# The last 255 attention logits moved to the border of two PSUM banks, and the padded column set by GpSimd, in a planned two-layer graph kernel

## The chip, the cores and the metric

The kernel runs on one core of one Trainium2 chip. The metric is the device time of one execution in microseconds, as the median of three runs. All arithmetic that this document speaks of is in fp32.

## The reference

The input is a matrix `x` of 3327 nodes by 256 features and a weighted adjacency matrix `adj` of 3327 by 3327. Two layers follow one another, each with a layer norm and a ReLU in front and a residual addition behind. The first one is what the change touches:

```python
def _top_p_attention(X, W1, W2, W3):
    q = X @ W1.T @ W2.T                    # 3327 x 64
    k = X @ W3.T                           # 3327 x 64
    logits = q @ k.T / TAU
    probs = jax.nn.softmax(logits, axis=-1)
    idx = jnp.argsort(-probs, axis=-1)
    sp = jnp.take_along_axis(probs, idx, axis=-1)
    cs = jnp.cumsum(sp, axis=-1)
    keep_sorted = cs - sp < TOP_P          # 0.9
    ...
    A = probs * mask
    return A / jnp.maximum(A.sum(-1, keepdims=True), 1e-12)
...
for n in range(STEPS):                     # 2
    A = _top_p_attention(Xa, W1, W2, W3)
    Xf = R @ Xf                            # R: row-normalised adj + I
    Xa = A @ Xa
    Z = Z + Xf @ U1[n].T + Xa @ U2[n].T
```

So for every node there are 3327 logits against all nodes; their exponentials are thinned to the largest that hold 0.9 of the sum, and what is left weighs the rows of `Xa`. The second layer is a graph attention with four heads over the neighbours that `adj` names.

## The kernel before, in words

The 3327 nodes are padded to 3328 (`NP`), which is 26 row tiles (`NT`) of 128. Thus exactly one node, the last of the last tile, is padding, and in every row of logits there is exactly one padded column, number 3327 (`N`).

**One row tile of attention** is an object of class `Row` (from L854). Its pieces run on all engines. `logits` (L873) makes the 128 x 3327 logits on TensorE in four portions of up to 1024 columns. Only 64 features are contracted, so the keys `kt` lie in two halves of the partitions: portion k holds 512 keys in partitions 0 to 63 and another 512 in partitions 64 to 127, and two matmuls (r = 0 and r = 1, L882) of 64 rows each fill the two banks of a PSUM tile `pl` of two banks. The last portion, k = 3, has only 255 columns: 128 for r = 0 at the start of the first bank, and 127 for r = 1 at the start of the second. For the padded 128th column of the second bank there is one more matmul, L890, of one column: its operands come from a constant tile `none` and make a logit of -32,000, whose exponential is zero. `exps` (L893) then takes one activation per portion on ScalarE, from PSUM to the SBUF tile `e` of 3328 columns, with the sum beside it; for k = 3 it reads 2 x 128 columns.

After that come the sum (`row_sum`), a guess of the threshold (`root` on GpSimd, `guess` and `density` on ScalarE), two or three counts over the 3327 columns on ScalarE (`count`, L933) with small steps on GpSimd or VectorE between them (`step`), a windowed search for the largest values on VectorE (`window`, L981; `sort`; `choose`, L1013), two small GpSimd operations between them (`free`, L995, lines L997 and L998), and four passes over `e` on VectorE that zero what falls below the threshold (`drop`, L1040). All of these read or write columns below 3327 only. Then TensorE transposes `e` in seven groups (`turn`, L1051; transposes at L1056), six of four and the last of two 128 x 128 blocks: the last transposed block, columns 3200 to 3327, holds the padded column. ScalarE copies each group out of PSUM (`turned`, L1061), and TensorE multiplies the blocks with the features (`attend`, L1068). Both steps have 26 such row tiles, 52 in all.

**Beside the attention** each step has 26 products with rows of the adjacency matrix (class `Full`: `some`, L1100, 26 matmuls of 128 x 128 by 256 or 257, fed by loads on SP's queue; `copy`, L1107, takes the result out of PSUM on ScalarE), and projections at the start (`project_u`, L1218) and after each row tile (`finish1`, `finish2`). The second layer's main loops are L1644 (VectorE), L1632 and L1633 (ScalarE), L1660 and L1674 (TensorE).

**The order of all this** is not written out by hand. Class `Plan` (L470) holds pieces, each with an engine, a length in microseconds that the author put in, a rank, the pieces it needs, and the buffers it takes and gives back. `order` (L497) simulates the five engines with these lengths: whenever an engine is free, it takes the piece of lowest rank among those whose needs and buffers are there. `issue` then emits the instructions in that order, and on the chip each engine works through its own queue in it. A length is thus no time on the chip, but it decides which piece comes before which, on all engines. The two logits pieces of a row (portions 0 and 1, then 2 and 3) are put at L1429 to L1431 with lengths 2.1 and 1.4, `free` at L1459 with length 0.8 (on GpSimd). Some pieces do nothing and only pass a buffer on; the one at L1223, put once for each of 26 tiles in `project_u`, has length 0.0 and lag 0.0 on SP.

In `order`, what a piece releases goes into a heap of events with a time (`finish`, L502). The loop handles all events up to the current time, lets each engine take a piece, and then moves the clock to the earliest later time at which an engine with waiting pieces is free, or at which the first event of the heap is due:

```python
times = [t for e, t in now.items() if t > clock and ready[e]] + ([events[0][0]] if events else [])
later = [t for t in times if t > clock]
```

Of the kernel before, what the change touches and what calls it, by code (L numbers as in the profile page):

```python
# [10 lines left out]
F32 = mybir.dt.float32  # L11
# [8 lines left out]
P = 128  # L20
N = 3327
# [3 lines left out]
DA = 64  # L25
# [444 lines left out]
class Plan:  # L470
# [26 lines left out]
    def order(self):  # L497
        free, events = dict(self.free), []
        now = dict.fromkeys(self.LAG, 0.0)
        ready = {e: [] for e in self.LAG}  # L500

        def finish(p, end):  # L502

            heapq.heappush(events, (end, p["k"], p, "own"))
            heapq.heappush(events, (end + p["lag"], p["k"], p, ""))
            for b in p["give"]:
                heapq.heappush(events, (end + p["lag"], p["k"], p, b))

        for k, p in enumerate(self.pieces):
            p["k"], p["left"], p["from"] = k, len(p["needs"]), 0.0  # L510
            if not p["left"]:
                ready[p["engine"]].append(p)
        out, clock, holds = [], 0.0, []
        while len(out) < len(self.pieces):
            while events and events[0][0] <= clock:
                _, _, p, what = heapq.heappop(events)
                if what == "end":

                    held = sum(max(0.0, min(z, clock) - max(a, p["at"])) for a, z in holds[-12:])
                    end = p["at"] + p["length"] + held  # L520
                    if end > clock + 1e-6:
                        now[p["engine"]] = end
                        heapq.heappush(events, (end, p["k"], p, "end"))
                    else:
                        finish(p, clock)
                    continue
                if what not in ("", "own"):
                    free[what] += 1
                    continue
                for q in p["then"]:  # L530
                    if (q["engine"] == p["engine"]) == (what == "own"):
                        q["left"] -= 1
                        if not q["left"]:
                            ready[q["engine"]].append(q)
            for e, queue in ready.items():
                if now[e] > clock or not queue:
                    continue
                can = [p for p in queue if all(free[b] >= p["take"].count(b) for b in p["take"])]
                if not can:
                    continue  # L540
                p = min(can, key=lambda q: q["rank"])
                queue.remove(p)
                for b in p["take"]:
                    free[b] -= 1
                p["at"] = clock
                now[e] = clock + p["length"]
                if p["hold"]:
                    holds.append((clock, clock + p["hold"]))
                if e == "POOL":
                    heapq.heappush(events, (now[e], p["k"], p, "end"))  # L550
                else:
                    finish(p, now[e])
                out.append(p)
            times = [t for e, t in now.items() if t > clock and ready[e]] + ([events[0][0]] if events else [])
            later = [t for t in times if t > clock]
            if not later:
                if len(out) < len(self.pieces):
                    raise RuntimeError("the plan stands still")
                break
            clock = min(later)  # L560
        self.end = max(now.values())
        return out
# [8 lines left out]
def fast(  # L571
# [59 lines left out]
    with ExitStack() as l0:  # L631
# [16 lines left out]
        kt = wpool.tile([P, 3 * 512 + P], F32, name="kt")  # L648
        qq = wpool.tile([P, NT, P], F32, name="qq")


        none = wpool.tile([P, P + 2], F32, name="none")
        GP.memset(none, 0.0)
        GP.memset(none[DA : DA + 32, :P], 1.0)
        GP.memset(none[DA : DA + 32, P:], -1.0e3)
        kks = [wpool.tile([P, P + 2], F32, name=f"kk{k}") for k in range(2)]
        for kk in kks:
            GP.memset(kk[:, :: P + 1], 1.0)
# [195 lines left out]
        class Row:  # L854
# [18 lines left out]
            def logits(self, k):  # L873

                if k == 0:
                    self.open()
                pl = ps_l.tile([P, 2, 512], F32, name="pl")
                w = 512 if k < 3 else P
                for r in range(2):
                    m = min(w, N - 1024 * k - w * r)  # L880
                    half = slice(r * DA, r * DA + DA)
                    T.matmul(  # L882
                        pl[:, r, :m],
                        qq[half, self.i, :],
                        kt[half, 512 * k : 512 * k + m],
                        start=True,
                        stop=True,
                    )
                    if m < w:
                        T.matmul(pl[:, r, m:w], none[half, :P], none[half, P : P + w - m], start=True, stop=True)  # L890
                self.pl[k] = pl[:, :, :w]

            def exps(self, k):  # L893
                pl = self.pl.pop(k)
                w = pl.shape[2]
                S.activation(  # L896
                    self.e[:, 1024 * k : 1024 * k + 2 * w].rearrange("p (r w) -> p r w", r=2),
                    pl,
                    AF.Exp,
                    accum_out=(self.p0, self.p1, self.p2, self.p3)[k],  # L900
                )
# [93 lines left out]
            def free(self):  # L995

                GP.tensor_scalar(self.room, self.h0, self.h1, self.b, ALU.add, ALU.subtract)  # L997
                GP.tensor_scalar(self.rec, self.s, self.h0, self.h1, ALU.subtract, ALU.subtract)  # L998

            def sort(self):  # L1000

# [417 lines left out]
        def search(row, rank, keys, stats_of, fresh):  # L1419


            n, i = row.n, row.i
            got, a = [], None
            for g in range(2):

                def logits(g=g):
                    row.logits(2 * g)
                    row.logits(2 * g + 1)

                a = plan.put(  # L1430
                    "PE", 2.1 - 0.7 * g, rank - 2.5, logits, needs=[keys, fresh, a], take=["pl", "pl"] + ["e", "sc"] * (1 - g)  # L1431
                )
                for k in (2 * g, 2 * g + 1):
                    got.append(
                        plan.put("ACT", 1.15 if k < 3 else 0.5, rank - 2.5, row.exps, k, needs=[a], give=["pl"])
                    )
            row.pieces = dict(logits=a)
            a = plan.put("ACT", 0.35, rank - 2.4, row.row_sum, needs=[got])
            a = plan.put("POOL", 1.3, rank - 2.4, row.root, needs=[a, stats_of])
            a = row.pieces["guess"] = plan.put("ACT", 1.0, rank - 2.4, row.guess, needs=[a])  # L1440
            more = plan.put("ACT", 0.85, rank - 2.2, row.density, needs=[a])
            for j in range(2):
                got = [
                    plan.put("ACT", 3.05, rank - (2.1, 1.7)[j], row.count, j, fn, needs=[a])
                    for fn in (AF.Relu, AF.Sign)[j:]
                ]
                a = plan.put("POOL", (3.8, 4.7)[j], rank - (2.0, 1.6)[j], row.step, j, GP, needs=[got, more])
            if EVALS[n] == 3:
                a = row.pieces["counted"] = plan.put("ACT", 3.05, rank - 1.4, row.count, 2, AF.Sign, needs=[a])
                a = plan.put("DVE", 2.7, rank - 1.3, row.step, 2, V, needs=[a])  # L1450
            halves = []
            for h in range(2):
                for part in range(2):
                    a = plan.put(
                        "DVE", 3.2 - 2.0 * part, rank - 1.0, row.window, h, part, needs=[a], take=["y"] * (1 - part),
                        give=["y"] * part, lag=0.02, hold=1.95 * (1 - part),
                    )
                    halves.append(a)
            may = plan.put("POOL", 0.8, rank - 1.5, row.free, needs=[halves[2]])  # L1459
            a = plan.put("DVE", (1.8, 2.5)[n], rank - 1.0, row.sort, needs=[a])  # L1460
            a = plan.put("DVE", 3.1, rank - 1.0, row.choose, needs=[a, may], take=["cum"])
            total = plan.put("POOL", 1.2, rank - 1.0, row.total, needs=[a], give=["cum"])
            drops = []
            for o in range(4):
                a = plan.put("DVE", 1.03, rank - 1.0, row.drop, o, needs=[a], hold=1.0)
                drops.append(a)
            return total, drops
# [504 lines left out]
```

## Time and profile before

| what | value |
|---|---|
| median of 3 runs | 2207.8 us (2207.56 to 2210.33) |
| the profiled execution: its own time | 2208.77 us |
| the profiled execution: its span in the trace | 2207.0 us |
| instructions in the trace | 35945 |
| VectorE busy | 1614.3 us (73%) |
| ScalarE busy | 1443.2 us (65%) |
| GpSimd busy | 932.8 us (42%) |

The span is from the first to the last instruction of the program in the trace; 1.77 us of the execution's own time lie around it. A group line of the profile names the source line, the engine, the operation, the written and read tiles, the shape and the count, then the summed busy time, the mean duration of one in ns, and the idle time before them with what ended it. PE is TensorE's matmuls, PEld its weight loads, DVE VectorE, ACT ScalarE, POOL GpSimd, SP the engine that issues DMAs. An fp32 matmul of the program shows up as two matmul instructions, called passes below, so that 52 matmuls of the source are 104 in the trace; the transposes at L1056 show up once.

By place, the attention steps with their adjacency products fill the trace up to about 1720 us, the second layer the rest: the first second-layer matmul at L1660 starts at 1722.25 us.

### The profile page before, as it was taken

What the parts mean: (1) busy time and instruction counts of PE and PEld (TensorE: products, weight loads), DVE (VectorE), ACT (ScalarE), POOL (GpSimd) and SP (SyncE); (2) the same over time, 40 slices, a digit from 0 to 9 for tenths busy, and PEclk for the clock granted to TensorE, in tenths of its full rate; (3) what the DMA queues carried; (4) which work ended last, traced back from release to release, by engine and by line L of the source; (5) the groups of instructions that cost most, each with busy time, mean ns of one, the idle gap of its engine ahead of it and who ended that gap; (6) DMA issues with size and microseconds to landing.
All of it is one profiled execution on the core that took longest, in us unless ns stands there. A gap on an engine that the chain in (4) does not pass through costs nothing. (4 is left out here: it accounts for less than half of the span.)

```text
span 2207.0 us, 35945 instructions
## 1 busy us (share of the span) xinstructions
PE 2169.5 (98%) x11978; PEld 1530.4 (69%) x11978; DVE 1614.3 (73%) x4229; ACT 1443.2 (65%) x2726; POOL 932.8 (42%) x2210
## 2 busy tenths in 40 slices
PE   8999999999999999999999999999999999999997
PEld 6488778778877788878777888878888433333332
DVE  5566757546665573177979798787778997989896
ACT  5776776566666751478787878778764555455553
POOL 5554465435454550255665656666663100000001
PEclk9999999999999999999999999999999999999999
DMA  4012121212212232532212222222224444444341
GB/s 120 1 45 85 49 70 50 75 52 61 73 49 76 65 92 80 185 84 63 67 55 62 60 72 71 77 63 63 71 77 143 137 126 138 116 141 124 110 128 52
DMA packets 192323, 183.75 MB, mean 83 GB/s; under 512 B 15386, under 2 KB 146176, under 8 KB 192128
## 3 DMA queue, kind: packets, MB, share of 16 engines
q1 hardware_dynamic: 191232, 181.15, 28.3%
q8 instruction: 96, 1.57, 0.3%
q14 instruction: 99, 0.81, 0.1%
q10 hardware_dynamic: 896, 0.21, 0.0%
HBM read 164.41 MB, written 15.94 MB: 82 GB/s over the span
## 5 line engine op out<-in xcount | busy, mean ns | idle before, releaser
L1068 PE MATMUL acca<-rhs,et 128*128 128x256 f32 x2704 | 616.8, 379 | 0.0
L933 ACT ACTIVATE junk<-e,sc 128x3327 fp8e5<-128x3327 f32 x182 | 559.0, 3071 | 68.3 <-POOL sc L978 67.6
L1068 PEld LDWEIGHTS acca<-rhs,et 128*128 128x128 f32 x2704 | 499.3, 190 | 62.5 <-issue 1.5
L1100 PE MATMUL accf<-c,at 128*128 128x256 f32 x1352 | 316.8, 383 | 4.7 <-ACT f L1107 4.5
L1100 PE MATMUL accf<-main,at 128*128 128x257 f32 x1352 | 310.9, 381 | 1.0 <-ACT f L1107 0.5
L988 DVE SCALAR_TENSOR_TENSOR y<-e,sc 128x1664 f32<-128x1664 f32 x104 | 208.9, 2009 | 131.6 <-POOL sc L975 129.6
L1100 PEld LDWEIGHTS accf<-c,at 128*128 128x128 f32 x1352 | 248.7, 190 | 51.0 <-issue 10.6
L1100 PEld LDWEIGHTS accf<-main,at 128*128 128x128 f32 x1352 | 250.8, 190 | 46.1 <-issue 9.4
L1061 ACT COPY et<-px 128x512 f32<-128x512 f32 (+1 forms) x364 | 192.3, 553 | 125.0 <-PE px L1056 69.8
L993 DVE MAX8 cands<-y 128x8 f32<-128x208 f32 x832 | 242.2, 361 | 3.6
L1043 DVE SCALAR_TENSOR_TENSOR e<-e,thr 128x832 f32<-128x832 f32 x208 | 213.0, 1079 | 1.8
L896 ACT ACTIVATE e<-pl 128x1024 f32<-128x1024 f32 x208 | 179.8, 868 | 42.0 <-PE pl L882 41.7
L1633 ACT ACTIVATE et<-at 128x448 bf16<-128x448 f32 (+1 forms) x204 | 112.3, 550 | 129.1 <-DVE e L1644 75.8
L1056 PE MATMUL px<-ident,e 128*128 128x128 f32 x1352 | 190.8, 274 | 5.4 <-ACT et L1061 2.5
L1796 POOL TENSOR_TENSOR qq<-qq 128x256 f32<-128x256 f32 x4 | 3.0, 754 | 452.3 <-ACT qq L1792 452.2
L1660 PE MATMUL pl<-e,main 128*64 128x416 f32 x1024 | 191.3, 517 | 0.2
L1056 PEld LDWEIGHTS px<-ident,e 128*128 128x128 f32 x1352 | 159.4, 141 | 45.4 <-issue 13.5
L882 PE MATMUL pl<-kt,qq 64*128 64x512 f32 (+1 forms) x832 | 173.5, 535 | 0.0
L1660 PEld LDWEIGHTS pl<-e,main 128*64 128x64 f32 x1024 | 70.8, 137 | 112.2 <-issue 87.1
L1644 DVE SCALAR_TENSOR_TENSOR e<-c,low,et 128x832 f32<-128x832 f32 x128 | 128.5, 1072 | 8.6 <-PE accf L1674 7.0
L882 PEld LDWEIGHTS pl<-kt,qq 64*128 64x128 f32 x832 | 71.6, 186 | 83.6 <-issue 80.3
L1644 DVE SCALAR_TENSOR_TENSOR e<-qq,low,et 128x832 f32<-128x832 f32 x120 | 120.5, 1075 | 6.0 <-PE accf L1674 4.4
(528 smaller groups left out, 3080.0 us busy)
## 6 DMA issues: line engine op xcount, KB each, us to landing
at<-in_adjt_dram SPq DMA_DIRECT2D x414, 256.0 KB
at<-in_adjt_dram SPq DMA_DIRECT2D x102, 192.0 KB
at<-in_adjt_dram SPq DMA_DIRECT2D x52, 128.0 KB
ys<-ystage SPq DMA_DIRECT2D x26, 256.0 KB
rhs<-in_x_dram SPq DMA_DIRECT2D x26, 128.0 KB
ystage<-in_x_dram SPq DMA_DIRECT2D x26, 128.0 KB
base<-ys SPq DMA_DIRECT2D x26, 128.0 KB
x1s<-ystage SPq DMA_DIRECT2D x26, 128.0 KB
```

Source lines behind the costliest of these rows:

```text
L882: T.matmul(pl[:, r, :m], qq[half, self.i, :], kt[half, 512 * k : 512 * k + m], start=True, stop=True,)
L896: S.activation(self.e[:, 1024 * k : 1024 * k + 2 * w].rearrange("p (r w) -> p r w", r=2), pl, AF.Exp, accum_out=(self.p0, self.p1, self.p2 ...
L933: S.activation(junk[:, :N], self.e[:, :N], fn, bias=t, scale=-1.0, accum_out=dst, saturate=False)
L988: V.scalar_tensor_tensor(self.y[:, : hi - lo], self.e[:, lo:hi], self.up, self.e[:, lo:hi], ALU.is_lt, ALU.mult, accum_out=(self.h0, self. ...
L993: V.max(self.cands[:, o // PIECE, :], self.y[:, o - lo : min(o + PIECE, hi) - lo])
L1043: V.scalar_tensor_tensor(piece, piece, self.thr[:, o : o + 1], piece, ALU.is_gt, ALU.mult)
L1056: T.transpose(pt[:, k, :], self.e[:, j * P : (j + 1) * P], ident)
L1061: S.copy(self.et[g][:, :m, :], self.pt.pop(g)[:, :m, :])
L1068: T.matmul(self.acc, et[:, j - 4 * g, :], rhs[self.n][:, j, :], start=(j == 0), stop=(j == NT - 1))
L1100: T.matmul(self.acc[:, : self.w], self.at[j // JC][:, j % JC, :], self.src[:, j, : self.w], start=(j == 0), stop=(j == NT - 1),)
L1644: V.scalar_tensor_tensor(held["e"][:, k, :], extra["both"][b % 2][:, k, :], low[:, j, k : k + 1], held["mask"], ALU.max, ALU.mult,)
L1660: T.matmul(q["acc"][a][k * FH : (k + 1) * FH, c, :C], main[:, j, h * FH : (h + 1) * FH], held["e"][:, h, c * C : (c + 1) * C], start=(j == 0),
```

## The change

The change has four parts. The one-column matmul at L890 and the constant tile `none` with its three memsets go. The last portion of logits lies differently in its PSUM tile: the 128 columns of r = 0 are the last 128 of the first bank, and the 127 of r = 1 the first 127 of the second, so that the 255 columns lie one behind the other across the border of the banks, and the activation reads 255 columns as one stretch (the other portions lie as before). Since nothing writes column 3327 of `e` any more, GpSimd sets it to zero at the end of `free`. In the plan, the lengths of the two logits pieces become 2.0 and 1.2, and `order` handles events that fall due at the current time before it moves the clock.

```diff
--- before.py
+++ after.py
@@ -551,6 +551,8 @@
                 else:
                     finish(p, now[e])
                 out.append(p)
+            if events and events[0][0] <= clock:
+                continue
             times = [t for e, t in now.items() if t > clock and ready[e]] + ([events[0][0]] if events else [])
             later = [t for t in times if t > clock]
             if not later:
@@ -648,11 +650,6 @@
         kt = wpool.tile([P, 3 * 512 + P], F32, name="kt")
         qq = wpool.tile([P, NT, P], F32, name="qq")
 
-
-        none = wpool.tile([P, P + 2], F32, name="none")
-        GP.memset(none, 0.0)
-        GP.memset(none[DA : DA + 32, :P], 1.0)
-        GP.memset(none[DA : DA + 32, P:], -1.0e3)
         kks = [wpool.tile([P, P + 2], F32, name=f"kk{k}") for k in range(2)]
         for kk in kks:
             GP.memset(kk[:, :: P + 1], 1.0)
@@ -876,25 +873,25 @@
                     self.open()
                 pl = ps_l.tile([P, 2, 512], F32, name="pl")
                 w = 512 if k < 3 else P
+
+                pl = pl.rearrange("p r w -> p (r w)")
                 for r in range(2):
                     m = min(w, N - 1024 * k - w * r)
                     half = slice(r * DA, r * DA + DA)
+                    lo = 512 - w + w * r
                     T.matmul(
-                        pl[:, r, :m],
+                        pl[:, lo : lo + m],
                         qq[half, self.i, :],
                         kt[half, 512 * k : 512 * k + m],
                         start=True,
                         stop=True,
                     )
-                    if m < w:
-                        T.matmul(pl[:, r, m:w], none[half, :P], none[half, P : P + w - m], start=True, stop=True)
-                self.pl[k] = pl[:, :, :w]
+                self.pl[k] = pl[:, 512 - w : lo + m]
 
             def exps(self, k):
                 pl = self.pl.pop(k)
-                w = pl.shape[2]
                 S.activation(
-                    self.e[:, 1024 * k : 1024 * k + 2 * w].rearrange("p (r w) -> p r w", r=2),
+                    self.e[:, 1024 * k : 1024 * k + pl.shape[1]],
                     pl,
                     AF.Exp,
                     accum_out=(self.p0, self.p1, self.p2, self.p3)[k],
@@ -996,6 +993,8 @@
 
                 GP.tensor_scalar(self.room, self.h0, self.h1, self.b, ALU.add, ALU.subtract)
                 GP.tensor_scalar(self.rec, self.s, self.h0, self.h1, ALU.subtract, ALU.subtract)
+
+                GP.memset(self.e[:, N:], 0.0)
 
             def sort(self):
 
@@ -1428,7 +1427,7 @@
                     row.logits(2 * g + 1)
 
                 a = plan.put(
-                    "PE", 2.1 - 0.7 * g, rank - 2.5, logits, needs=[keys, fresh, a], take=["pl", "pl"] + ["e", "sc"] * (1 - g)
+                    "PE", 2.0 - 0.8 * g, rank - 2.5, logits, needs=[keys, fresh, a], take=["pl", "pl"] + ["e", "sc"] * (1 - g)
                 )
                 for k in (2 * g, 2 * g + 1):
                     got.append(
```

## The prediction, made before the changed kernel was run

> **What bounds the kernel now.** I read the first part of the page, then busy time by stage, then TensorE's waits, and then single instructions.
>
> ```profile
> PE 2169.5 (98%) x11978; PEld 1530.4 (69%) x11978; DVE 1614.3 (73%) x4229; ACT 1443.2 (65%) x2726; POOL 932.8 (42%) x2210
> ```
>
> Busy time by stage (columns: stretch, its length, then PE, PEld, DVE, ACT and POOL busy, clock, DMA share, GB/s):
>
> ```profile
> 60.00:120.00 60.00, 55.74 (x192) 29.41 (x193) 38.78 (x117) 45.78 (x86) 29.83 (x73) 1.00 0.00 1
> 120.00:1720.00 1600.00, 1588.89 (x8074) 1289.82 (x8073) 1101.97 (x3445) 1105.38 (x1929) 854.38 (x2008) 1.00 0.26 74
> 1720.00:2180.00 460.00, 459.83 (x3323) 169.07 (x3325) 431.04 (x492) 248.33 (x597) 6.87 (x6) 1.00 0.43 126
> ```
>
> TensorE is busy in 1588.9 of the 1600 us of the attention steps and in 459.8 of 460 us of layer 2, while no other engine is above 69% (1105/1600) in the steps. So TensorE's queue sets the time from 60 us to the end: what it is spared arrives at the end, unless a wait takes its place. VectorE, at 431 of 460 in layer 2, is close behind there, but its last row tile hangs on TensorE's logits, so both begin layer 2 earlier together. TensorE's waits between 120 and 1720 us (engine, line, who it waited for: us, times, longest):
>
> ```profile
> PE accf L1100 <- ACT f L1107: 5.1, 11, 1.1
> PE px L1056 <- ACT et L1061: 2.5, 4, 0.8
> PE px L1056 <- DVE gk L792: 2.1, 1, 2.1
> PE px L1056 <- DVE e L1043: 0.7, 2, 0.5
> PE accf L1100 <- DMA at<-in_adjt_dram: 0.4, 1, 0.4
> ```
>
> All stalls there are 11.1 us (1600 - 1588.9), and 4.3 us between 60 and 120. That is all that a better order could win, 15.4 us.
>
> The instructions concerned, by shape:
>
> ```profile
> L882 PE MATMUL pl<-kt,qq 64*128 64x512 f32 x624 | 162.0, 624 | 0.0
> L882 PE MATMUL pl<-kt,qq 64*128 64x128 f32 x104 | 19.8, 270 | 0.0
> L882 PE MATMUL pl<-kt,qq 64*128 64x127 f32 x104 | 19.8, 270 | 0.0
> L890 PE MATMUL pl<-none 64*128 64x1 f32 x104 | 14.5, 207 | 0.0
> ```
>
> The L890 row tempts one to book 14.5 us. But matmuls overlap and their ends are modelled; what counts is how much later the next one starts. From the timeline of one row near 1540 us, first portions 0 and 1, then 2 and 3, TensorE alone (start, length, x passes):
>
> ```profile
> 1536.82 0.60 PE L882 MATMUL pl<-kt,qq 64*128 64x512 f32 x2
> 1537.25 0.60 PE L882 MATMUL pl<-kt,qq 64*128 64x512 f32 x2
> 1537.77 0.48 PE L1100 MATMUL accf<-c,at 128*128 128x256 f32 x1
> ...
> 1542.63 0.39 PE L882 MATMUL pl<-kt,qq 64*128 64x128 f32 x4
> 1542.74 0.28 PE L882 MATMUL pl<-kt,qq 64*128 64x128 f32 x2
> 1542.86 0.28 PE L890 MATMUL pl<-none 64*128 64x1 f32 x2
> 1543.07 0.48 PE L1100 MATMUL accf<-c,at 128*128 128x256 f32 x1
> ```
>
> Two things are to be seen. The passes of r = 0 and r = 1 start together in pairs, 0.43 us apart for 512 columns (1536.82 to 1537.25) and 0.11 us for 128 (1542.63 to 1542.74). And the change from 64-row matmuls back to 128-row ones has a price of its own: the last wide pair should be through at 1537.25 + 0.43 = 1537.68, but the next matmul starts at 1537.77, 0.09 us later.
>
> **What the Trainium skill says.** "TensorEngine Tiling (Array Packing)", Key Properties: changing the tiling mode drains TensorE, and different tiles work in parallel. The trace agrees: paired starts, and the 0.09 us on the way out. The same page, Instruction Overhead: each matmul has some 60 cycles of overhead, and one with a free dimension of 1 takes as long as one of 60. Here the two passes of L890 start 0.03 us apart (at 1542.86 and 1542.89), against 0.11 us for 128 columns, so the floor is small beside the drain. "SBUF — State Buffer", Who interferes with whom: a VectorE instruction with two SBUF inputs holds up a GpSimd instruction that reads SBUF, not one that only writes it. The trace shows the first half (GpSimd operations of 0.3 to 0.6 us last 1.94 us beside the drops near 1517 us); that a memset is spared, no run shows yet.
>
> **The change part by part.**
>
> The one-column matmul. With it, the next work starts at 1543.07, 0.33 us after the last real pair at 1542.74. Without it I expect the pair's own 0.11 us and the same 0.09 us for the change of mode: 0.20 us. That is 0.12 to 0.13 us a row; taking medians over all 52 rows from the starts of passes, 0.318 us becomes 0.107 + 0.092 = 0.199, so 0.119 us. Both weight loads of `none` go too, but they lie inside this stretch. Sum: 52 x 0.119 = **6.2 us**, all on the path. The ends: if something of about 0.18 us (1543.07 - 1542.89, last L890 pass to the next kind) must follow any short last pass in place of 0.09, counted from the r = 1 pass that starts at 1542.75 and holds its rows for 0.11, the saving is only 0.03 us a row, 1.6 us; if the 0.18 us counts from that pass's start, it is 0.32 - 0.18 = 0.14 us, 7.3 us.
>
> The three memsets of `none` lie at 1.1 to 1.95 us on GpSimd, which then idles 1.15 us until VectorE's first statistics at 3.79 us: nothing.
>
> Two banks in place of two. The two matmuls write to different banks as before. The activation of 256 columns takes 386 ns (x52); one column less is at most 52 x 0.001 us on ScalarE, which has room, and three of its four activations already run over both banks as one stretch: nothing. ScalarE gets portion 3 about 0.12 us earlier: also off the path.
>
> The memset on GpSimd. Not in the trace in this place; the nearest rows are memsets of the start, 0.10 us for 128 x 1 and 0.14 us for 128 x 26. 52 x 0.1 = 5 us on an engine that is 42% busy. Queued behind it are steps of other rows, on which ScalarE's counts wait (67.6 us of such waits in all); 0.1 us more in each of two or three steps a row delays the search, which has slack: TensorE waits for its result (L1043) 0.7 us in all. Bounds: zero, and up to 52 x 2 us of GpSimd time if VectorE locks it out after all (the longest L1047 took 2.09 us), still within the slack that the next paragraph shows for TensorE.
>
> The new wait. The 26th transposed block reads column 3327, so TensorE now waits there for GpSimd. Over the 52 rows, the time from the end of L998 to the start of that transpose is 14.3 us at least, 26.6 us at the median; the memset follows L998 directly, so the wait is met long before. All of TensorE's queue stands behind it, so it would matter if it were not. Its form matters more: on this kernel's weight loads the trace shows one wait each, and a second one is a separate semaphore instruction (51 ns, L1056 has 55 of them, nearly all at the first group of a row), after which the next matmul starts 0.31 to 0.37 us after the one before instead of 0.22. In the groups 1, 3 and 4 the trace shows a second wait carried by a later block's own weight load, with no loss (starts 109 ns apart with and without). The last group has a wait on its first block, and the new one falls on its second, which has none: cost zero. The upper end: 52 x 0.13 = 6.8 us, which would eat the gain.
>
> The plan. The new lengths make 3.2 us of a row's logits where the chip took 1.918 + 1.397 = 3.315 us and should take 3.196; before it was 3.5. So the plan comes closer to the chip. With 52 x 0.3 us less on TensorE, and px released in time 26 times in `project_u` (the only pieces of length and lag zero: L1223), the simulated clock shifts against all others, and pieces change places on all queues, by fractions of a microsecond at first. On SP and GpSimd too, whose loads and steps may come a place earlier or later. No row of the trace prices this. Its ends: the better side is at most the 15.4 us of stalls, and half of them, 7.7, is already much; on the worse side there is no bound but the stalls per event, 0.46 us at a change of the `accf` bank. I take zero, as TensorE's stalls are already 0.7% of the steps and either sign is open.
>
> **Sum** against the profiled execution: 2208.8 - 6.2 = 2202.6 us; it is 1.0 us above the median of the runs, so against that 2207.8 - 6.2 = **2201.6 us**.
>
> **The rivals.**
>
> (1) The order turns out better: with px seen in time and logits costed right, half of the 15.4 us of stalls go: 2207.8 - 6.2 - 7.7 = 2193.9. For it: 4.3 us lie between 60 and 120 us, just where L1218 waits and the simulation was late. Against it: the stalls are many small ones with different releasers.
>
> (2) The gain of the matmul is smaller or paid back in form: the drain stays 0.18 us (saving 1.6 us: 2206.2), or a semaphore instruction comes at each last group (6.8 against 6.2: 2208.4). For it: the price of a short last pass without L890 is nowhere in the trace. Against it: the waits carried by later blocks.
>
> (3) The order turns out somewhat worse and gives back half: 2204.7. For it: any change of lengths shuffles a plan whose TensorE has almost no slack left to lose less.
>
> (4) Slower: in the new order the next adjacency product follows its predecessor too closely. Each changeover at which its first matmul is at once next in TensorE's queue waits for ScalarE's copy (L1107) to free the bank: 5.1 us / 11 = 0.46 us. Now 11 of the 52 changeovers do; break-even is at 6.2 / 0.46 = 13 or 14 more, and 35 in all cost 24 x 0.46 = 11.0: 2207.8 - 6.2 + 11.0 = 2212.6. From there on it is slower. Against it: the pieces of `full` have ranks that change little.
>
> That the change does not do what it says has no case: the column that was made zero by an exponential is made zero by a memset, and the rest reads columns below it.
>
> **How the numbers follow.** Forecast 0.46 at 2201.6, its own spread 2198 to 2203.4; (1) 0.15; (2) 0.10; (3) 0.18; (4) 0.11. About 0.2% (4.4 us) is what a measurement of this kernel can tell from no change: faster is below 2203.4, slower above 2212.2. Faster: 0.46 + 0.15 = 0.61. Same: 0.10 + 0.18 = 0.28. Slower: 0.11. The range goes from (1) at 2193 up to 2210, over (2) and (3), and leaves out (4) and little else.
>
> **What would show it.** In the changed profile: no L890; the next matmul 0.20 us after the last 127-column pair; a memset of about 0.1 us after L998, with no wait of TensorE for it; the semaphore instructions at L1056 still about 55; TensorE's busy time in the steps shorter by about 6 us, its stalls about 11 and 4 us. The prediction is wrong if those stalls change by more than 3 us, if the exit after the short pair stays above 0.25 us, or if layer 2 does not move up by what the steps won.

## The result, and the profile after

The changed kernel takes 2201.95 us (median of 9 runs, 2201.09 to 2204.53), the kernel before beside it 2208.8 us (9 runs): a ratio of 0.9971, 95% interval 0.9962 to 0.998, or 6.8 us less. The forecast was 2201.6 us, 6.2 below a median of 2207.8. So the number came out, but the experiments below show that it did so by luck, by two errors of about the same size: the one-column product was worth less than its 6.2 us, and the new order, taken at zero, brought the rest.

First the lines that answer to those of before: the engines' busy time on the page, and the stages (stretch, length, then PE, PEld, DVE, ACT, POOL).

```profile
PE 2163.6 (98%) x11874; PEld 1522.6 (69%) x11874; DVE 1612.5 (73%) x4229; ACT 1444.8 (66%) x2726; POOL 929.9 (42%) x2259
```

```profile
60.00:120.00 60.00, 55.13 (x186) 28.72 (x187) 38.70 (x117) 46.10 (x85) 29.97 (x75) 1.00 0.00 1
120.00:1720.00 1600.00, 1588.30 (x8002) 1285.01 (x8002) 1102.68 (x3450) 1108.03 (x1933) 854.02 (x2058) 1.00 0.26 74
1720.00:2180.00 460.00, 459.75 (x3340) 167.90 (x3338) 429.63 (x488) 247.49 (x593) 4.53 (x5) 1.00 0.43 126
```

TensorE has 104 passes fewer (11978 to 11874) and is still at work in nearly all of every stage. Its stalls are 60 - 55.13 = 4.9 us and 1600 - 1588.30 = 11.7 us, against 4.3 and 11.1 before. The span went from 2207.0 to 2201.8 us. The profiled execution took 2203.67 us, 1.7 above the median of its runs, so the profile shows 5.1 us of the 6.8; where the other 1.7 us lie, it can't say.

The end of a row's logits on TensorE (start, length, passes):

```profile
1560.70 0.28 PE L882 MATMUL pl<-kt,qq 64*128 64x128 f32 x2
1560.91 0.48 PE L1099 MATMUL accf<-c,at 128*128 128x256 f32 x1
```

From the last short pair to the next matmul it is now 0.21 us by these rounded starts, in place of 0.33; by medians over the 52 rows, from the very last pass, 0.202 in place of 0.320 us. The memset in the groups by shape:

```profile
L997 POOL MEMSET e<- 128x1 f32 x52 | 5.1, 98 | 0.0
```

52 memsets of 98 ns in the mean (93 to 102), and no instruction of any engine is recorded as having waited for one. TensorE's waits between 120 and 1720 us:

```profile
PE accf L1099 <- ACT f L1106: 5.9, 11, 1.1
PE px L1055 <- ACT et L1060: 3.6, 2, 3.3
PE px L1055 <- DVE e L1042: 1.0, 3, 0.5
PE accf L1099 <- DMA at<-in_adjt_dram: 0.7, 1, 0.7
```

The total is nearly the old one, but one wait is new, a single 3.3 us for `et`, and one is gone, the 2.1 us for `gk` (near 438 us in the kernel before). Both are followed up below.

### The profile page after: what moved, and what is told of

Its sections match the earlier page's. It is cut to its first block, busy times and chain, and to the rows that moved or that the text cites. A ratio compares the mean times of both kernels' runs of the same rounds, so it can differ in the third digit from the quotient of the medians.

```text
span 2201.8 us, 35765 instructions
## 1 busy us (share of the span) xinstructions
PE 2163.6 (98%) x11874; PEld 1522.6 (69%) x11874; DVE 1612.5 (73%) x4229; ACT 1444.8 (66%) x2726; POOL 929.9 (42%) x2259
```

## The experiments

All ratios are to the kernel before, with 95% intervals; medians in us.

| kernel | product | order | median | ratio |
|---|---|---|---|---|
| changed kernel | no | new | 2201.95 | 0.9971 (0.9962 to 0.998) |
| e1_old_plan | no | old | 2206.16 | 0.9988 (0.9982 to 0.9995) |
| e2_plan_only | yes | new | 2206.47 | 0.9989 (0.9983 to 0.9996) |
| e3_extra_one | one, unread | new | 2206.17 | 0.9988 (0.9981 to 0.9994) |
| e4_extra_two | two, unread | new | 2215.47 | 1.0031 (1.0019 to 1.0043) |
| e5_zero_once | no | new | 2202.94 | 0.997 (0.996 to 0.9981) |
| e6_late_fill | no | new | 2202.65 | 0.9972 (0.9961 to 0.9983) |
| e7_fix_only | no | loop new, lengths old | 2205.43 | 0.9985 (0.9978 to 0.9991) |
| e8_len_only | no | loop old, lengths new | 2204.18 | 0.9979 (0.9972 to 0.9987) |
| f3_short (threshold cut short) | no | old | 2214.86 | 1.0028 (1.0017 to 1.0039) |
| f4_short_product (threshold cut short) | yes | old | 2216.87 | 1.0037 (1.0023 to 1.0051) |
| e9_exact_len | no | 1.92 and 1.28 | 2202.16 | 0.9972 (0.9962 to 0.9982) |
| f2_mixed_len | no | 2.1 and 1.2 | 2202.0 | 0.9972 (0.9961 to 0.9983) |

The kernel before took 2208.73 us beside e1 to e4, 2209.0 beside e5 to e8, and 2208.97 beside f2 to f4 and e9.

**The product in the old order (e1).** The changed kernel with the plan of before:

```diff
-            if events and events[0][0] <= clock:
-                continue
...
-                    "PE", 2.0 - 0.8 * g, rank - 2.5, logits, ...
+                    "PE", 2.1 - 0.7 * g, rank - 2.5, logits, ...
```

> The changed kernel with the plan of before: lengths 2.1 and 1.4, and the event loop as it was, so that all pieces stand in the order of before. My theory (the one-column product costs 0.119 us of TensorE's queue in each of 52 rows, and the order matters little): 6.2 us below the kernel before, about 2202.6, and the next matmul after the short pair 0.20 us behind its last start. The rival (the new order made the gain): within 1 us of the kernel before, about 2208.8. If both contribute, between the two.

Measured: 2206.16, only 2.6 us below the kernel before (1.1 to 4.0 by the interval). Between the two theories, so neither alone.

A part of the shortfall goes with the granted TensorE clock, of which each execution has its mean on record: 16 of e1's 21 executions lie at 0.997 or lower, and only 18 of the 58 of the kernel before. At 0.998, e1 is 3.9 us ahead by means (2204.58 in 4 executions against 2208.44 in 40), at 0.997 it is 3.6 us (2206.29 in 9 against 2209.91 in 17). So 2.6 to 3.9 of the 6.2 us arrive, but in no comparison all of them.

This run is worth a closer look, because its 11,874 matmuls stand in exactly the order of the kernel before (without L890). So one can go through both traces (whose clock is 1.00 from 19 us to the last 12 us) matmul by matmul and note by how much e1 is ahead at each start. A selection, in us:

| before, start | e1 is ahead by |
|---|---|
| 117.5 | -0.1 |
| 447.1 | 0.8 |
| 747.2 | 1.9 |
| 808.2 | 1.6 |
| 1442.1 | 2.9 |
| 1712.2 | 2.8 |
| 2190.9 | 2.8 |

In nearly every row the lead grows by 0.119 us behind the short pair. But it is also given back. Sorting all changes of the lead by the matmul at which they happen and by what it waited for gives, for the profiled executions: gained after the short pairs 6.0 us; given back 0.3 net before 120 us, where the start-up differs; 1.0 net in the first step, 0.9 of it at first matmuls of an adjacency product that wait for ScalarE's copy (L1107, L1104 in e1); and 1.9 in the second step, of which 0.8 at the first transposes of a row, which wait for VectorE's drops. Sum: 6.0 - 0.3 - 1.0 - 1.9 = 2.8. From about 1450 us on, every row gains 0.119 at its logits and returns about as much at its next transpose: there TensorE was no longer ahead of a search that VectorE, GpSimd and ScalarE finish just in time. TensorE's waits between 120 and 1720 us in e1, for comparison with the five lines of before:

```profile
PE accf L1097 <- ACT f L1104: 6.5, 14, 1.1
PE px L1053 <- ACT et L1058: 2.7, 4, 0.9
PE px L1053 <- DVE gk L787: 2.3, 1, 2.3
PE px L1053 <- DVE e L1040: 0.9, 2, 0.6
```

14 waits for `f` in place of 11, and 6.5 us in place of 5.1. The stages say the same in one number: stalls of 13.1 us (1600 - 1586.92) in place of 11.1.

**The order alone (e2).** The kernel before with the new lengths and the new event loop, everything else as it was.

```diff
+            if events and events[0][0] <= clock:
+                continue
...
-                    "PE", 2.1 - 0.7 * g, rank - 2.5, logits, ...
+                    "PE", 2.0 - 0.8 * g, rank - 2.5, logits, ...
```

> The kernel before with the plan of the changed kernel alone: lengths 2.0 and 1.2 and the event loop that handles due events first; the one-column product, the layout and the exponential stay. My theory: no change, 2208.8 within 1.5 us. The rival (the order made the gain): about 2202. A third possibility, that the new order costs something which the product hides in the changed kernel: above 2210.3.

Measured: 2206.47, 2.3 us below the kernel before. So the order does count, by about a third of the whole.

**The product in the new order (e3, e4).** One or two unread one-column products in each row of the changed kernel:

```diff
+                    if m < w:
+                        T.matmul(pl[:, lo + m : lo + m + 1], none[half, :P], none[half, P : P + 1], start=True, stop=True)
                 self.pl[k] = pl[:, 512 - w : lo + m]
```

> The changed kernel with one more product of one column in each row, into the free PSUM column behind the 255 logits, which nobody reads; all else, order and memset too, as in the changed kernel. My theory: the price comes back in full, 6.2 us above the changed kernel, about 2208.2, and 0.32 us from the last real pass to the next matmul. The rival (the product hid in the change of mode, and the gain is of the order or the layout): within 1 us of the changed kernel, about 2202.

Measured: 2206.17, 4.2 us above the changed kernel, between the theories again, and as e2, which has the same order and a product too. The stretch after the last real pass is 0.320 us again. The matmuls of e2 and e3 stand in the same order, and what separates the two kernels is the layout, the column set by memset and the new wait: together 0.3 us, nothing that can be told from noise.

> The changed kernel with two such unread products of one column in each row. If each product costs what its weight load and pass take, two cost twice one: about 12.4 us above the changed kernel, 2214.4. If only the first costs, because it stretches the change of mode once, the second adds at most 0.03 to 0.06 us a row (2 to 3 us): about 2210 to 2211.

Measured: 2215.47, 13.5 us above the changed kernel and 9.3 above e3, with 0.544 us after the last real pass. The second product costs TensorE 0.224 us a row, nearly twice the first; of these 11.6 us in 52 rows 9.3 arrive. So neither case of the expectation came true: the sum of 13.5 is near the 12.4 of the first, but the two products cost different amounts. In the trace of e4:

```profile
1637.26 0.25 PE L894 MATMUL pl<-none 64*128 64x1 f32 x1
1637.37 0.36 PE L895 MATMUL pl<-none 64*128 64x1 f32 x2
...
1637.48 0.25 PE L895 MATMUL pl<-none 64*128 64x1 f32 x1
1637.66 0.48 PE L1106 MATMUL accf<-c,at 128*128 128x256 f32 x1
```

The one-column passes of a further product follow one another by 0.11 us (1637.26, 1637.37, 1637.48), as 128 columns do. Their weight loads start 0.112 us apart too, and each of these passes 0.03 us behind its load: each pass loads its 128 weight columns anew, and that, not its one column, is its price. That the passes write the same column is not the reason, as the two of the first product do so 0.03 us apart. The Trainium skill, "TensorE: Matmul & The Clock Gate", LDWEIGHTS, has nearly the same: a load takes the number of weight columns divided by 1.2, in ns, which is 107 for 128 (the record of one load here lasts 188 ns, but they overlap). The first product is cheaper because one of its two loads runs while the last real passes do: it starts at 1637.12, as the last of these passes does.

**The memset and its wait (e5, e6).**

```diff
-                GP.memset(self.e[:, N:], 0.0)
...
+        for _ in range(BUFS["e"]):
+            GP.memset(epool.tile([P, NP], F32, name="e")[:, N:], 0.0)
```

> The changed kernel without the memset in each row: the padded column of each of the four buffers of e is set to zero once at the start, since no later row writes it before the second layer; TensorE's last transpose no longer waits for GpSimd. My theory (the memset and its wait are hidden): within 1.5 us of the changed kernel, about 2202. The rival (the new wait or the 52 memsets cost something): 2 to 7 us less, 2195 to 2200.

In e6 the memset stands at the end of `total` in place of `free`:

> The changed kernel with the memset moved from the end of free to the end of total, which GpSimd can only begin when VectorE has chosen the threshold, some 4 us and more before TensorE's last transposes. My theory (26 us of slack at the median in the old place): the slack shrinks by about 10 us but stays above zero in most rows, so within 1.5 us of the changed kernel. If GpSimd runs later than that, its queue holds up TensorE: each wait of 1 us in 52 rows would cost up to 52 us, and the time shows it.

Measured: 2202.94 and 2202.65, 1.0 and 0.7 us above the changed kernel, inside the intervals. Neither taking the memsets and their wait away nor moving the wait nearer changes the time: both were hidden. In e6 the way from the memset to the transpose that needs it shrinks from 27 to 14 us at the median, and TensorE waits for the memset once, 0.4 us.

**Which part of the plan (e7, e8), and other lengths (e9, f2).** The edits are the event loop or the lengths alone, as in the diffs above.

> The changed kernel with the lengths of before (2.1 and 1.4) but the event loop of the changed kernel. My theory: the order matters little, about 2202 within 2 us. The rival (the event loop frees the start, where 4.9 us of TensorE's stalls lie between 60 and 120 us): as fast as the changed kernel, while the same without the event loop is slower by 2 us or more.

> The changed kernel with its lengths (2.0 and 1.2) but the event loop of before. My theory: about 2202 within 2 us. The rival: if the lengths, nearer to the measured 1.92 and 1.28 us, bring a better order, this is as fast as the changed kernel, and with the old lengths slower by 2 us or more.

Measured, all without the product: neither 2206.2 (e1), the event loop alone 2205.4, the lengths alone 2204.2, both 2202.0. The intervals of e7 and of e1 overlap, so that the loop alone brings anything isn't shown, nor that it adds something to the new lengths (e8 against the changed kernel); by itself it moves only 12 of the 11,874 matmuls, all before 50 us. The lengths alone bring some 2 us: the intervals of e8 and e1 overlap too, but drawing anew from the executions of both gives 0.8 to 3.7 us as a 95% interval of the difference itself.

> The changed kernel with the logits' lengths in the plan as measured: 1.92 and 1.28 in place of 2.0 and 1.2. If nearness to the chip makes the order better, this is below the changed kernel, by up to the 3.3 us that it loses in one stall near 1575 us: 2199 to 2201. If an order's quality is chance at this grain, it lies anywhere between 2200 and 2207.

> The changed kernel with the first length of before and the second of after: 2.1 and 1.2. If the second length brings the gain of the order, as fast as the changed kernel, 2202; if both are needed, 2204 to 2206; if an order's quality is chance at this grain, anywhere between 2200 and 2207.

Measured: 2202.16 and 2202.0, as the changed kernel. Lengths nearer to the chip (e9) thus bring nothing; f2 came out as in the case that the second length brings the gain, but chance would allow it too. With the new event loop, three of four pairs of lengths give 2202 and the old pair 2205.4. The profile of f2 has the fewest stalls of all from 60 to 1720 us:

```profile
60.00:120.00 60.00, 57.10 (x200) 30.54 (x200) 40.88 (x125) 45.40 (x83) 31.23 (x79) 1.00 0.00 1
120.00:1720.00 1600.00, 1591.71 (x8020) 1283.94 (x8023) 1106.69 (x3448) 1106.55 (x1936) 866.13 (x2056) 1.00 0.25 74
```

2.9 and 8.3 us; its span was 2198.5 us, but its median shows no gain over the changed kernel. No version clearly beats the changed kernel.

**Is it VectorE that takes the gain back? (f3, f4)** The choice of the threshold cut short by nine small VectorE instructions and one on GpSimd, in the old order, without and with the product (part of the edit):

```diff
-                V.scalar_tensor_tensor(out_, win, nxt, keep, ALU.is_gt, ALU.mult, accum_out=self.cnt)
...
-                V.tensor_scalar(self.thr, upto, 1.0 - 2.0**-24, nxt, ALU.add, ALU.mult)
+                V.tensor_scalar(self.thr, nxt.to_broadcast([P, 4]), 1.0 - 2.0**-24, None, ALU.mult)
```

> The changed kernel with the plan of before, and the choice of the threshold on VectorE cut short: the handling of equal values at the threshold (nine small VectorE instructions of a row, some 2 us, and one on GpSimd) is left out; the plan keeps its lengths, so the order stays that of before. It is to be read against the next run, which differs from it only by the one-column product and what belongs to it. My theory: in the second step each row's 0.119 us was taken back where TensorE waits for VectorE's drops; with VectorE done 2 us earlier those waits go, and the difference to the next run grows from 2.6 us to 4 to 6 us. The rival (something else takes the gain back): the difference stays at 2 to 3 us.

> The kernel before, product and layout and all, with the same cut of the choice on VectorE (the handling of equal values at the threshold is left out). My theory: TensorE has 0.7 us of waits for the drops in the kernel before, so this is 0 to 3 us below it. The rival (VectorE sets the pace of the second step): 10 us and more below it.

Both expectations failed. With less work on VectorE, both kernels are slower than before, by 5.9 and 7.9 us, and the product's price is 2.0 us by medians, no larger than the 2.6 of e1.

The pair doesn't decide its question, though. The 7 and 5 executions spread over 4 us each, and those of f3 have the lower clock (0.993 to 0.996 against 0.996 to 0.998); at 0.996 the difference is 3.5 us (2 against 4 executions). In both traces TensorE's waits for the drops are gone, and matmul by matmul f3 gives back 0.8 of the 3.1 us that it gains in the second step, where e1 gave back 1.9. That speaks for the theory, from one execution each.

Why both are slower is plainer. Compared matmul by matmul with the kernel before (same order), f4 loses 2.5 us at 98 us, at a projection that waits for ScalarE, and 2.4 us each near 1087 and 1198 us, at transposes that wait for ScalarE's copy `et`. The place near 1087 us in f4, on GpSimd, then ScalarE:

```profile
1083.68 0.96 POOL L970 TENSOR_SCALAR sc<-sc 128x1 f32<-128x1 f32 x1
1084.72 1.27 POOL L947 TENSOR_TENSOR sc<-sc,powers 128x1 f32<-128x1 f32 x1
1086.10 1.94 POOL L972 TENSOR_SCALAR sc<-sc 128x1 f32<-128x1 f32 x1
```

```profile
1089.03 3.07 ACT L934 ACTIVATE junk<-e,sc 128x3327 fp8e5<-128x3327 f32 x1 [3.78 <-POOL sc L979]
...
1092.10 1.05 ACT L1052 COPY et<-px 128x512 f32<-128x512 f32 x2
```

The drops of VectorE (L1035 in f4) run there from 1083.51 to 1087.6. Earlier by some 2 us in the row, they now fall on a GpSimd step: its operations take 0.96, 1.27 and 1.94 us, where the same ones took 0.19 to 0.55 us before. ScalarE's count waits for that step, 3.78 us in place of 1.37, then counts for 3.07 us, and only behind it in ScalarE's queue is the copy that TensorE needs. The places at 98 and 1198 us have the same make, and so has the new 3.3 us stall of the changed kernel:

```profile
1566.59 1.33 POOL L943 TENSOR_TENSOR sc<-sc,powers 128x1 f32<-128x1 f32 x1
1568.03 2.93 POOL L968 TENSOR_SCALAR sc<-sc 128x1 f32<-128x1 f32 x1
```

```profile
1571.95 3.07 ACT L930 ACTIVATE junk<-e,sc 128x3327 fp8e5<-128x3327 f32 x1 [5.46 <-POOL sc L975]
...
1575.02 0.56 ACT L1060 COPY et<-px 128x512 f32<-128x512 f32 x1
```

```profile
1575.63 1.67 PE L1055 MATMUL px<-ident,e 128*128 128x128 f32 x8 [3.30 <-ACT et L1060]
1577.09 1.92 PE L1099 MATMUL accf<-c,at 128*128 128x256 f32 x4
```

VectorE's drops run from 1566.42 to 1570.9 there. It is no accident of one execution: the profiles of e2, e3, e5, e6 and e8, all with lengths 2.0 and 1.2, have a stall of 3.2 to 3.3 us at the same place, that of e4 one of 2.9; those of e1 and e7, with the old lengths, have none over 1.5 us after 440 us and before layer 2.

The stall costs more than its 3.3 us, because the granted clock, the third number from the end, drops behind it:

```profile
1576.00:1579.40 3.40, 3.40 (x14) 2.94 (x13) 3.05 (x11) 2.55 (x7) 0.00 (x0) 0.50 0.02 4
```

In e4, whose matmuls come in the same order and whose clock stays at 1.00 here, the same eight transposes and four products take 1.09 and 1.03 us in place of 1.67 and 1.92:

```profile
1586.50 1.09 PE L1062 MATMUL px<-ident,e 128*128 128x128 f32 x8 [2.94 <-ACT et L1067]
1587.42 1.03 PE L1106 MATMUL accf<-c,at 128*128 128x256 f32 x4
```

Start by start, the stretch costs 1.7 us, so the new order loses 5.0 us here. In f4 two such stretches, behind the stalls near 1087 and 1198 us, cost 1.2 and 1.7 us more. What the new order wins is in part the wait of 2.1 to 2.3 us for `gk` near 438 us: the traces of the kernel before, e1, e7, f3 and f4, all with lengths 2.1 and 1.4, have it, those with other lengths don't. Where it wins the rest stays open.

## Why the prediction was right, and where it was not, step by step

**The price of the product on TensorE** was right to the nanosecond: 0.119 us a row, 1.398 to 1.279 us for portions 2 and 3, with the 0.09 us of the change of mode staying. Neither end of its bounds came up. Its reason was less right: the product's weight loads, set aside as lying inside the stretch, are what it costs (e4).

**"All on the path" failed.** Of 6.2 us, 2.6 arrive in the old order (e1; 3.6 to 3.9 at equal clock) and 4.2 in the new (e3 against the changed kernel). The page's 98% and the stalls of 11 us were read as if TensorE alone set the pace and a shorter TensorE would leave the stalls as they are; the proviso "unless a wait takes its place" was there, but priced at nothing. In e1's trace the gain is lost where another engine's chain is already level with TensorE, and there 0.1 us gained becomes 0.1 us more of waiting. The waits that I listed as what a better order could win were also the list of where a gain is lost: 1.9 us in the second step, the largest part at the drops, whose 0.7 us I had called slack.

**"The plan: I take zero" failed too**, by 2.3 us with the product in place (e2) and 4.2 without (changed kernel against e1). It lies within the bounds given, and the sign is that of rival (1), at a third to a half of its size. That the lengths are nearer to the chip isn't shown to be the reason: 1.92 and 1.28 are nearer still and give the same, as 2.1 and 1.2 do, of which the first is no nearer. Apart from the wait for `gk`, why the order with the old pair is the poorer one stays open, and that the order of the changed kernel is better at all is luck as far as the prediction goes.

The two errors cancel. Taking the product out first, 2.6 us (e1) and then 4.2 for the order make the 6.8 that was measured; taking the order first, 2.3 (e2) and then 4.5 for the product. For the profiled executions the sum closes in another form: 5.88 us less busy time and 0.75 us more idle time of TensorE make 5.13 us of span. Of the signs that the prediction named for being wrong, those on the stalls and on the exit after the short pair did not come up: stalls that barely change in all can hold one error and its opposite.

**The memset, the wait and its form** were right: 98 ns; TensorE never waits for it; the semaphore instructions at the transposes are 50 (55 before), so the new wait rides on a weight load as forecast. e5 and e6 bear it out. **The three memsets of `none`** and **the layout** have no run of their own; the layout is in the 0.3 us between e2 and e3, the activation of 255 columns lasts 0.38 us at the median in place of 0.39, and nothing in the start-up points to the memsets.

**Rival (2)**'s cases, a longer drain and a semaphore instruction, are excluded by the trace. **Rival (4)** named a real place: waits at changeovers of `accf` are what e1 gives back in the first step. But in the changed kernel they are 11, as before, and the longest stall of the new order is another one, the 3.3 us chain from the drops through GpSimd and ScalarE.

Layer 2 begins at 1718.60 in place of 1722.25 us, 3.7 us earlier, while the end moved by 5.1: in the new order less of the steps' work is left behind the first product of layer 2, 6 passes of projections in place of 12. That it "moves up by what the steps won" was thus too simple a test.

## What to carry to other kernels

A queue that is busy 98% of the time is not the only bound: take the waits that it still has as places where a gain will be given back, and when the order of the work can be held fixed, compare the two traces start by start, which shows where each tenth of a microsecond goes. Split a change that also re-plans into its local part and its order with two kernels, before believing a sum that came out right. A step on an engine of little load can sit between two loaded ones: shortening VectorE's work here cost 6 to 8 us, as at three places long VectorE passes came to lie on a GpSimd step on which ScalarE, and behind it TensorE, waits. And before reading differences of 2 or 3 us, compare the mean clocks of the executions.

## What the runs showed of the hardware that was not expected

A second one-column matmul with weights of its own costs as much as one of 128 columns, 0.224 us for its two passes, the pace of the weight loads.

A long stall of TensorE can have a stretch of half clock behind it. In the 14 traces, all nine stalls of 3.0 us and more after 90 us have a stretch of 3.4 or 6.8 us at a granted clock of 0.50 that begins within 1.5 us of their end, and of the ten from 2.1 to 2.9 us three have one; between 90 us and the last 15 us of the span there is no other. In such a stretch of the changed kernel transposes start 0.213 us apart, in place of 0.109. No run varies the length of a stall by itself, so where the limit lies isn't shown.

GpSimd operations that read SBUF last up to 2.93 us beside VectorE's drops in place of some 0.34 us, but the six memsets of e6 that lie within a drop take 93 to 96 ns. That agrees with what the Trainium skill states in "SBUF — State Buffer", Who interferes with whom, of GpSimd instructions that only write. The 52 memsets of the changed kernel don't test it, as none of them meets a drop.
